# First graph parts of layer 1 issued beside the last outputs of layer 0, and one PSUM pool for both layers

## The chip, the cores and the metric

The kernel runs on one core of one Trainium2 chip. The metric is the device time of one execution in microseconds (us). The kernel before was executed three times, and the median of those three is its time. A profiled execution was taken beside them, with a trace of the instructions of each engine: PE (TensorE; PEld is its weight loads), DVE (VectorE), ACT (ScalarE), POOL (GpSimd) and SP (SyncE, which here issues most DMAs).

## The reference

Two graph layers over N = 3327 nodes with D = 256 features, all in float32. The adjacency matrix `adj` is N x N, and its entries are 0 or 1.

```python
# layer 0: graph attention, 4 heads of 64
h = relu(layernorm(x))
support = (h @ weight) per head
logits[h, n, m] = f1[h, m] + f2[h, n]          # two inner products of support
attn = softmax over m of leaky_relu(logits, 0.2) where adj[n, m] != 0
x = x + attn @ support + bias + h @ proj_w.T + proj_b

# layer 1: two steps of a graph mean beside a top-p attention
h = relu(layernorm(x))
R = row-normalized (adj + I);  Xf = Xa = h;  Z = 0
for n in range(2):
    A = rows of softmax((Xa W1' W2') (Xa W3')'), cut to the largest entries
        that hold 0.9 of the row, normalized again
    Xf = R @ Xf
    Xa = A @ Xa
    Z = Z + Xf @ U1[n].T + Xa @ U2[n].T
out = x + layernorm(h + Z)
```

## The kernel before

**Tiles.** The nodes make NT = 26 row tiles of 128 (the last has 127), and seven groups of up to four tiles (NG = 7; the seventh has two).

**Layer 0** goes over four blocks of 1024 columns (the last has 255), and in each block over the 26 row tiles: 104 steps. A step loads a tile of the transposed adjacency on SP's queue, writes it back to DRAM in the kernel's own copy `adj_r` on POOL's queue, and DVE weighs it once for each of the four heads (`weigh`, L570). The weighed tiles are `w`, from a ring of seven buffers. PE sums features (L578) and weights (L588) of all rows in PSUM. At a block's end the sums are copied to `ot`, and each of the block's row tiles gets an `Out` object with these pieces of work: `divide` (PE turns `ot`, L437), `normalize` (DVE divides, adds the residual and takes the statistics of the layer norm, POOL the root, ACT writes h, L464), `turn` (PE transposes h, L473), `keys` (L483, then `take_keys`), `graph` (PE multiplies by U1, L506; ACT copies the sums into the resident `xf0` and into `xu`, which SP stores in `p_d`) and `take_graph` (DVE's low part of `xf0`, L517, and stores). The outputs of the first three blocks are spread over the steps of the following block. The last block has just two row tiles, 24 and 25, and their outputs stand behind the loop, L683 to L694, with nothing else beside them: both divides and normalizes, a mean of the keys known so far, both turns, both keys, both graph products.

**Layer 1** handles one row tile in one iteration n, for n = -3 to 28, twice (steps s = 0 and 1). Several row tiles are in work at the same time, in roles from `m3` (queries loaded) over `m` (logits in seven pieces, L799, copied from PSUM by ACT or DVE, L810; then one exponential over the row, L822), `a` (probes that seek the threshold, L880), `b` (keep, L985) and `c` (transposes, L998, copies, L1008, and products with the features, L1019) to `d`. Their order is written out by hand, in six strings called PLANS. The R @ Xf of the step is cut into parts: `graph(i, s, ...)` is a generator that yields seven parts for row tile i. Each part loads a 128 x 4 x 128 piece of `adj_r` (`adjt`, a ring of ADJ = 3, issued by SP at L722) and issues eight matmuls on it (L742 and L743: high and low half of the features). Part 0 has two more with the identity; part 6 has two adjacency tiles and four matmuls. In part 3 the ends of the row tile before are forced and `ad` is loaded from `p_d`.

Each token `graph` in a plan adds `parts(s, n) / fills` to an amount due, where `fills` is 7, and issues a part whenever a whole one is due. In step 0 the iterations n = -1, 0 and 1 issue 3, 7 and 8 parts; the rest of the 182 is spread evenly over the other 24 iterations:

```python
even = (NG * NT - sum(PARTS[s].values())) / (LAST[s] - 2)
```

**Order.** The instructions of PE, DVE, ACT and POOL keep the order in which they are written in the program (`in_traced_order`). SP's order is the scheduler's.

**PSUM** has eight banks. Layer 0 takes them by number, `bank(k)`, from a pool of its own (`ps1`). That pool is closed, and layer 1 opens another (`ps2`) with named rings: `lg` 3 banks (logits, and the small products and transposes of roles c and d), `tr` 2 (transposes), `acca` 1 (product), `accr` 2 (graph).

Of the kernel before, what the change touches and what calls it, by code (L numbers as in the profile page):

```python
# [10 lines left out]
FP = mybir.dt.float32  # L11
FR = mybir.dt.float32r
# [42 lines left out]
def kernel(  # L55
# [126 lines left out]
    def queries_and_keys(xt, i, s, ptag, keys):  # L182


        pn = rows(i)
        pq = ps.tile([P, P], FP, tag=ptag, name="pq", bufs=3)
        for c in range(DC):
            nc.tensor.matmul(
                pq[:, :pn], wqk[:, c, :], xt[:, c, :pn], start=(c == 0), stop=(c == DC - 1)
            )  # L190
        yield
        t = small.tile([P, 2, P], FR, tag="qk", name="qk", bufs=1)
        yield from hi_and_lo(t, pq, i, s)
        nc.sync.dma_start(
            out=qk_d[s][:, :, i * P : i * P + pn].rearrange("v a n -> a v n"),
            in_=t[:, :, :pn].bitcast(FP),
        )
        if keys:
            take_keys(keys, t, i)
        yield  # L200
# [95 lines left out]
    right = kept.enter_context(tc.tile_pool(name="right", bufs=1, side="right"))  # L296
    pq = right
    res = right.tile([P, NT, D], FP, tag="xa", name="res")
    xf0 = new_graph(right)
    keys = new_keys(right)  # L300
    first_traced = len(nc.cur_bb.bb.instructions)
    with ExitStack() as l0:
        p0 = l0.enter_context(tc.tile_pool(name="p0", bufs=1))
        pa = l0.enter_context(tc.tile_pool(name="pa", bufs=2))
        ps = l0.enter_context(tc.tile_pool(name="ps1", bufs=1, space=PSUM))

        def bank(k, shape):
            return ps.tile(shape, FP, tag=f"b{k}", name="pt")

# [283 lines left out]

        ats = {}
# [14 lines left out]
        for step, (b, j) in enumerate(order):  # L609
# [11 lines left out]
            )  # L621
            i = j + AHEAD
# [41 lines left out]
            if b < NB - 1:  # L664
                last = b == NB - 2
                for k, r in enumerate(outs):
                    a = step + 1 + 3 * k
                    ka, kb, kc = ((3, 4)[k % 2], (5, 6)[k % 2], 7) if last else (6, 7, 6)
                    g = a + 5
                    for when, f in (  # L670
                        (a, lambda r=r, ka=ka: r.divide(ka)),
                        (a + (3 if last else 2), lambda r=r, kb=kb: r.turn(kb)),
                        (a + (4 if last else 3), lambda r=r, kb=kb: r.keys(kb)),
                        (g, lambda r=r, kc=kc: r.graph(kc)),
                    ):
                        on_pe.setdefault(when, []).append(f)
                    for when, f in (
                        (a + 1, r.normalize),
                        (a + (5 if last else 4), r.take_keys),
                        (g + 1, r.take_graph),  # L680
                    ):
                        on_dve.setdefault(when, []).append(f)
        for k, r in enumerate(outs):  # L683
            r.divide(k)
            r.normalize()
        mean_of_keys(keys, 0)
        for k, r in enumerate(outs):
            r.turn(2 + k)
# [21 lines left out]

    def graph(i, s, xf, ends):


        pn, n0 = rows(i), i * P
        acc = ps.tile([P, DX], FP, tag="accr", name="accr")
        dx = D if s else DX
        for g in range(NG):
            c0 = 4 * g
            a = pw.tile([P, 4, P], FR, tag="adjt", name="adjt", bufs=ADJ)
            cn = min(4, NT - c0)  # L720
            nf = min(cn, NF - c0)
            nc.sync.dma_start(  # L722
                out=a[:, :nf, :pn].bitcast(FP),
                in_=adj_r[c0 * P : (c0 + nf) * P, n0 : n0 + pn].rearrange("(c p) n -> p c n", p=P),
            )
            if nf < cn:
                move_rows(
                    nc.sync, a[:, nf, :pn].bitcast(FP), adj_r[NF * P :, n0 : n0 + pn], rows(NF)
                )
            if g == 3:  # L730
                while ends:
                    ends.pop(0)[1]()
                ad = pw.tile([P, D], FP, tag="ad", name="ad", bufs=1)
                move_rows(nc.sync, ad, (z_d if s else p_d)[n0 : n0 + pn], pn)

            todo = [(a[: rows(c0 + j), j, :pn], c0 + j) for j in range(cn)]
            if g == 0:
                todo.insert(0, (ident_r[:pn, :pn], i))
            for n, (w, c) in enumerate(todo):
                begin, end = g == 0 and n == 0, g == NG - 1 and n == len(todo) - 1  # L740
                xc = xf[c // HB][: rows(c), c % HB]
                nc.tensor.matmul(acc[:pn, :dx], w, xc[:, :dx], start=begin, stop=False)  # L742
                nc.tensor.matmul(acc[:pn, :D], w, xc[:, DX:], start=False, stop=end)  # L743
            if g < NG - 1:
                yield

        def add():
            if s == 0:
                nc.vector.reciprocal(rdeg[:pn, i : i + 1], acc[:pn, D : D + 1])
            nc.vector.scalar_tensor_tensor(  # L750
                ad[:pn], acc[:pn, :D], rdeg[:pn, i : i + 1], ad[:pn], ALU.mult, ALU.add
            )
            if s == STEPS - 1:
                move_rows(nc.sync, r_d[n0 : n0 + pn], ad, pn)

        def high():
            nc.scalar.copy(hl[:pn, 0], ad[:pn])

        def low():
            nc.vector.tensor_tensor(hl[:pn, 1], ad[:pn], hl[:pn, 0].bitcast(FP), ALU.subtract)  # L760
            move_rows(nc.sync, xf_d[s + 1][n0 : n0 + pn], hl.bitcast(FP), pn)

        ends.append(("dve", add))
        if s < STEPS - 1:
            hl = pw.tile([P, 2, D], FR, tag="hl", name="hl", bufs=1)
            ends += [("act", high), ("dve", low)]
        yield
# [3 lines left out]
    class Rows:  # L771
# [20 lines left out]
        def logits(r, k_sb, *pieces):  # L792
            pn = r.pn
            for p in pieces:
                m0 = p * 512
                mn = min(512, N + 1 - m0)
                r.pg[p] = ps.tile([P, 512], FP, tag="lg", name="pg", bufs=3)
# [194 lines left out]
        def transpose(r, *groups):  # L992
            for g in groups:
                if g == 0:
                    r.pt, r.wt = {}, {}
                r.pt[g] = ps.tile([P, 4, P], FP, tag="tr", name="pt")
# [16 lines left out]
        def product(r, xa, *groups):  # L1013
            for g in groups:
                if g == 0:
                    r.acc = ps.tile([P, D], FP, tag="acca", name="acca", bufs=1)
# [27 lines left out]
        def features_t(r):  # L1044
            r.ft = ps.tile([P, DC, P], FP, tag="lg", name="pt", bufs=3)
# [13 lines left out]
        def small_products(r, u_sb):  # L1059
            r.pz = ps.tile([P, 2, D], FP, tag="lg", name="pz", bufs=3)  # L1060
# [198 lines left out]
    )  # L1259
    LAST = (NT, NT - 1)  # L1260

    def parts(s, n):
        if n in PARTS[s]:
            return PARTS[s][n]
        even = (NG * NT - sum(PARTS[s].values())) / (LAST[s] - 2)
        return even if n < LAST[s] else 0.0

    with ExitStack() as fast:
        ps = fast.enter_context(tc.tile_pool(name="ps2", bufs=2, space=PSUM))
# [10 lines left out]
        graph_ends = []  # L1280

        def parts_of_graph(s, xf):
            for i in range(NT):
                yield from graph(i, s, xf, graph_ends)
# [89 lines left out]
    with ExitStack() as gen:  # L1374
        ps = gen.enter_context(tc.tile_pool(name="ps3", bufs=2, space=PSUM))
        pf = ps.tile([1, 1], FP, tag="lg", name="pf", bufs=3)
# [11 lines left out]
        with tc.If(lost_v > 0):  # L1388
            for s in range(STEPS):
                with ExitStack() as st:  # L1390
                    pc = st.enter_context(tc.tile_pool(name=f"gc{s}", bufs=1))
                    pw = st.enter_context(tc.tile_pool(name=f"gw{s}", bufs=1))
                    pq = pw
# [83 lines left out]
```

## Time and profile before

| | us |
|---|---|
| median of three executions | 2097.78 |
| lowest and highest | 2092.39 and 2099.72 |
| profiled execution, its own time | 2095.06 |
| span of its trace | 2092.8 |
| PE busy | 1985.8 (95%) |
| DVE busy | 1715.9 (82%) |
| ACT busy | 1265.2 (60%) |
| POOL busy | 787.5 (38%) |

The mean granted clock of TensorE in the profiled execution is 0.984 of full speed. Times inside the trace count from the start of its span. Layer 0 ends and layer 1 begins around 684 to 700 us; the last graph part of step 0 starts its last matmuls at 1382 (PE's rows of L742), and step 1 lasts from there to the end. In the listings, `L742` is line 742 of the kernel, `out<-in` are the program's names, `x6` is a number of instructions, and brackets give the idle time of the engine just before and what ended it. The profile's page has the span in 40 equal slices, with the busy share of each engine in tenths:

```profile
## 2 busy tenths in 40 slices
PE   6999999999999679999999999998899999999996
...
DVE  4777888878877388888888888864899999999995
ACT  2110000000012588888888888847899999999982
```

### The profile page before, as it was taken

What the parts mean: (1) busy time and instruction counts of PE and PEld (TensorE: products, weight loads), DVE (VectorE), ACT (ScalarE), POOL (GpSimd) and SP (SyncE); (2) the same over time, 40 slices, a digit from 0 to 9 for tenths busy, and PEclk for the clock granted to TensorE, in tenths of its full rate; (3) what the DMA queues carried; (4) which work ended last, traced back from release to release, by engine and by line L of the source; (5) the groups of instructions that cost most, each with busy time, mean ns of one, the idle gap of its engine ahead of it and who ended that gap; (6) DMA issues with size and microseconds to landing.
All of it is one profiled execution on the core that took longest, in us unless ns stands there. A gap on an engine that the chain in (4) does not pass through costs nothing. (4 is left out here: it accounts for less than half of the span.)

```text
span 2092.8 us, 34266 instructions
## 1 busy us (share of the span) xinstructions
PE 1985.8 (95%) x11474; PEld 1387.5 (66%) x11474; DVE 1715.9 (82%) x4065; ACT 1265.2 (60%) x1940; POOL 787.5 (38%) x1834
## 2 busy tenths in 40 slices
PE   6999999999999679999999999998899999999996
PEld 3333223323333468888888888876798898888885
DVE  4777888878877388888888888864899999999995
ACT  2110000000012588888888888847899999999982
POOL 2330033223233233444444444432555444554441
PEclk9999999999999889999999999999899999999998
DMA  5455555655645433333333333377334443334420
GB/s 173 146 174 170 161 196 190 229 175 183 217 131 175 130 81 91 102 100 98 102 102 103 100 103 103 101 224 197 77 99 102 118 105 102 101 99 111 107 73 20
DMA packets 319569, 270.60 MB, mean 129 GB/s; under 512 B 30168, under 2 KB 293335, under 8 KB 319256
## 3 DMA queue, kind: packets, MB, share of 16 engines
q1 hardware_dynamic: 303480, 216.03, 37.7%
q0 software_dynamic: 14736, 51.62, 7.0%
q8 instruction: 92, 1.51, 0.3%
q14 instruction: 93, 0.76, 0.1%
q10 hardware_dynamic: 1168, 0.67, 0.1%
HBM read 177.79 MB, written 88.62 MB: 127 GB/s over the span
## 5 line engine op out<-in xcount | busy, mean ns | idle before, releaser
L880 ACT ACTIVATE junk<-lg,at 128x3327 fp8e4<-128x3327 f32 (+1 forms) x208 | 637.8, 3067 | 13.8 <-POOL at L846 11.2
L570 DVE SCALAR_TENSOR_TENSOR w<-xf,cf,at 128x1024 f32<-128x1024 f32 (+1 forms) x312 | 382.1, 1278 | 55.9 <-PE pt L588 55.9
L742 PE MATMUL accr<-xf,adjt 128*128 128x258 f32 (+3 forms) x1352 | 366.8, 304 | 19.3 <-DMA adjt<-adj_r 18.9
L578 PE MATMUL pt<-w,sup 128*64 128x512 f32 (+3 forms) x1456 | 341.0, 576 | 10.6 <-DVE w L570 8.5
L743 PE MATMUL accr<-xf,adjt 128*128 128x256 f32 (+1 forms) x1352 | 340.6, 284 | 0.0
L1019 PE MATMUL acca<-res,wt 128*128 128x256 f32 (+2 forms) x1352 | 319.3, 381 | 0.0
L1019 PE MATMUL acca<-xa,wt 128*128 128x256 f32 (+2 forms) x1352 | 315.1, 382 | 3.0 <-ACT wt L1008 3.0
L742 PEld LDWEIGHTS accr<-xf,adjt 128*128 128x128 f32 (+1 forms) x1352 | 259.0, 192 | 29.9 <-DMA adjt<-adj_r 14.3
L1019 PEld LDWEIGHTS acca<-xa,wt 128*128 128x128 f32 (+2 forms) x1352 | 251.1, 191 | 34.7 <-ACT wt L1008 3.5
L1019 PEld LDWEIGHTS acca<-res,wt 128*128 128x128 f32 (+2 forms) x1352 | 249.2, 191 | 30.8 <-issue 0.5
L743 PEld LDWEIGHTS accr<-xf,adjt 128*128 128x128 f32 (+1 forms) x1352 | 259.8, 192 | 5.6
L799 PE MATMUL pg<-k_sb,q 128*128 128x512 f32 (+2 forms) x728 | 242.5, 425 | 17.3 <-DVE lg L810 8.4
L578 PEld LDWEIGHTS pt<-w,sup 128*64 128x64 f32 (+1 forms) x1456 | 95.9, 136 | 221.4 <-issue 149.2
L820 POOL TENSOR_SCALAR sc<-sc 128x1 f32<-128x1 f32 (+1 forms) x156 | 29.2, 215 | 505.0 <-ACT sc L818 505.0
L998 PE MATMUL pt<-ident,e 128*128 128x128 f32 (+1 forms) x1352 | 193.4, 276 | 20.8 <-DVE e L985 13.5
L946 DVE MAX8 v<-lg 128x8 f32<-128x416 f32 (+2 forms) x416 | 210.0, 577 | 0.1
L998 PEld LDWEIGHTS pt<-ident,e 128*128 128x128 f32 (+1 forms) x1352 | 162.8, 144 | 61.2 <-ACT wt L1008 18.1
L937 DVE SCALAR_TENSOR_TENSOR lg<-e,th 128x3327 f32<-128x3327 f32 (+1 forms) x52 | 191.1, 3676 | 4.1 <-ACT th L930 4.1
L985 DVE SCALAR_TENSOR_TENSOR e<-e,vm 128x3327 f32<-128x3327 f32 (+1 forms) x52 | 191.2, 3677 | 0.1
L822 ACT ACTIVATE e<-lg,sc 128x3327 f32<-128x3327 f32 (+1 forms) x52 | 159.7, 3072 | 29.9 <-issue 27.4
L1008 ACT COPY wt<-pt 128x512 f32<-128x512 f32 (+2 forms) x268 | 142.6, 544 | 55.7 <-PE pt L998 39.0
L588 PE MATMUL pt<-w,eas 128*32 128x512 f32 (+3 forms) x1456 | 166.6, 569 | 0.0
(180 smaller groups left out, 2696.1 us busy)
## 6 DMA issues: line engine op xcount, KB each, us to landing
adjt<-adj_r SPq DMA_DIRECT2D x300, 256.0 KB, 3.2
at<-in_adj_t_dram SPq DMA_DIRECT2D x75, 512.0 KB, 3.8
adj_r<-at POOLq DMA_DIRECT2D x75, 512.0 KB, 4.7
qk_d<-qk SPq DMA_DIRECT2D x50, 128.0 KB, 2.2
q<-qk_d SPq DMA_DIRECT2D x100, 64.0 KB, 2.5
xf_d<-xf SPq DMA_DIRECT2D x50, 128.0 KB, 2.5
xf_d<-hl SPq DMA_DIRECT2D x25, 256.0 KB, 2.0
xf<-f_d SPq DMA_DIRECT2D x24, 256.0 KB, 4.9
```

The source lines that it names most:

```text
L570: nc.vector.scalar_tensor_tensor(o, cb, cf[:pj, j, h : h + 1], a, ALU.max, ALU.mult)
L578: nc.tensor.matmul(acc[q * O : (q + 1) * O, :mn], sup[:pj, j, h * O : (h + 1) * O], ws[h][:pj, 512 * m : 512 * m + mn], start=(j == 0), st ...
L588: nc.tensor.matmul(acc[h * QP : (h + 1) * QP, :mn], eas[:pj, j, h : h + 1].to_broadcast([pj, QP]), ws[h][:pj, 512 * m : 512 * m + mn], sta ...
L742: nc.tensor.matmul(acc[:pn, :dx], w, xc[:, :dx], start=begin, stop=False)
L743: nc.tensor.matmul(acc[:pn, :D], w, xc[:, DX:], start=False, stop=end)
L799: nc.tensor.matmul(r.pg[p][:pn, :mn], r.q[:, v, :pn], k_sb[:, m0 : m0 + mn], start=(v == 0), stop=(v == 1),)
L880: nc.scalar.activation(junk[:pn], r.lg[:pn, :N], AF.Exp, bias=r.at[:pn, 4:], accum_out=r.g[:pn], saturate=False,)
L937: nc.vector.scalar_tensor_tensor(r.lg[:pn, :N], e, r.th[:pn], e, ALU.is_lt, ALU.mult, accum_out=r.below[:pn])
L946: nc.vector.max(r.v8[:pn, q], r.lg[:pn, q * w : min((q + 1) * w, N)])
L985: nc.vector.scalar_tensor_tensor(e, e, r.vm[:pn, 1:], e, ALU.is_ge, ALU.mult, accum_out=kept[:pn])
L998: nc.tensor.transpose(r.pt[g][: rows(c), j, : r.pn], r.e[: r.pn, c * P : c * P + rows(c)], ident[: r.pn, : r.pn],)
L1019: nc.tensor.matmul(r.acc[: r.pn], wt[: rows(c), j, : r.pn], xa[: rows(c), c, :], start=(c == 0), stop=(c == NT - 1),)
```

## The change

There are three edits.

1. **One PSUM pool.** It is opened before layer 0. Layer 0 takes banks by number as before. Layer 1's rings are fixed banks in round robin, counted per kind, and every `ps.tile(..., tag="lg")` and the like becomes `psum("lg", ...)`.
2. **Parts begun early.** `graph` and the load of a part (`load_part`) are defined before layer 0. Behind the loop of layer 0, after the last divides and normalizes and the mean of the keys, six parts of row tile 0 and two of row tile 1 are issued, ahead of the last two turns. The loads of the first three are issued in the last step of the loop and take their buffers from the ring of `w`, as the five others do. For these two row tiles, the ends of the row tile before and the load of `ad` come in part 6 and no longer in part 3.
3. **Quota.** These eight parts are subtracted (`DONE`), so that the 24 iterations share 156 parts and no longer 164. The iterations n = -1, 0 and 1 keep 3, 7 and 8.

```diff
+    ps = kept.enter_context(tc.tile_pool(name="ps", bufs=1, space=PSUM))
+    def bank(k, shape):
+        return ps.tile(shape, FP, tag=f"b{k}", name="pt")
+    BANKS = {"lg": (2, 3, 4), "tr": (0, 1), "acca": (5,), "accr": (6, 7)}
+    used = dict.fromkeys(BANKS, 0)
+    def psum(what, shape):
+        k = BANKS[what][used[what] % len(BANKS[what])]
+        used[what] += 1
+        return bank(k, shape)
...
+    BEGUN = 2
+    adjs = {}
+    def load_part(i, g):
+        pn, n0, c0 = rows(i), i * P, 4 * g
+        a = new_adj()
...
     def graph(i, s, xf, ends):
...
-        acc = ps.tile([P, DX], FP, tag="accr", name="accr")
+        acc = psum("accr", [P, DX])
...
-            a = pw.tile([P, 4, P], FR, tag="adjt", name="adjt", bufs=ADJ)
+            a = adjs.pop((i, g), None) or load_part(i, g)
...
-            if g == 3:
+            if g == (NG - 1 if i < BEGUN else 3):
                 while ends:
                     ends.pop(0)[1]()
                 ad = pw.tile([P, D], FP, tag="ad", name="ad", bufs=1)
                 move_rows(nc.sync, ad, (z_d if s else p_d)[n0 : n0 + pn], pn)
...
-        ps = l0.enter_context(tc.tile_pool(name="ps1", bufs=1, space=PSUM))
...
+        def new_adj():
+            return pa.tile([P, 4, P], FR, tag="w", name="adjt", bufs=7)
...
+            if step == len(order) - 1:
+                for g in range(3):
+                    adjs[0, g] = load_part(0, g)
             i = j + AHEAD
             weigh(j, at, b, cn, 0, 1)
...
+        graph_ends = []
+        begun = [graph(i, 0, xf0, graph_ends) for i in range(BEGUN)]
         for k, r in enumerate(outs):
             r.divide(k)
             r.normalize()
         mean_of_keys(keys, 0)
+        for part in range(EARLY // 4):
+            next(begun[0])
+        for part in range(2):
+            next(begun[1])
         for k, r in enumerate(outs):
             r.turn(2 + k)
...
-                r.pg[p] = ps.tile([P, 512], FP, tag="lg", name="pg", bufs=3)
+                r.pg[p] = psum("lg", [P, 512])
...
-                r.pt[g] = ps.tile([P, 4, P], FP, tag="tr", name="pt")
+                r.pt[g] = psum("tr", [P, 4, P])
...
-                    r.acc = ps.tile([P, D], FP, tag="acca", name="acca", bufs=1)
+                    r.acc = psum("acca", [P, D])
...
+    DONE = (EARLY // 4 + 2, 0)
...
-        even = (NG * NT - sum(PARTS[s].values())) / (LAST[s] - 2)
+        even = (NG * NT - DONE[s] - sum(PARTS[s].values())) / (LAST[s] - 2)
...
-        ps = fast.enter_context(tc.tile_pool(name="ps2", bufs=2, space=PSUM))
...
+        def new_adj():
+            return pw.tile([P, 4, P], FR, tag="adjt", name="adjt", bufs=ADJ)
 
         def parts_of_graph(s, xf):
             for i in range(NT):
-                yield from graph(i, s, xf, graph_ends)
+                yield from graph(i, s, xf, graph_ends) if s or i >= BEGUN else begun[i]
```

## The prediction, on record before the result

> **What bounds the kernel now.** I read the page's 40 slices first (layer 0 ends in slice 13, layer 1 begins), then one-microsecond windows and the timelines there, then the tile period behind it. The chain of waits reaches back only to 1487 us and says nothing of this place.
>
> Windows around the seam (columns: stretch, length, busy time of PE, PEld, DVE, ACT, POOL, granted clock, DMA share, GB/s):
>
> ```profile
> 684.00:685.00 1.00, 0.53 (x5) 0.33 (x4) 0.70 (x4) 0.00 (x0) 0.00 (x0) 1.00 0.79 266
> ...
> 687.00:688.00 1.00, 0.00 (x0) 0.00 (x0) 0.86 (x5) 0.28 (x1) 0.57 (x2) 0.96 0.00 0
> 688.00:689.00 1.00, 0.63 (x2) 0.29 (x2) 0.98 (x2) 0.32 (x1) 0.61 (x2) 0.50 0.00 0
> ...
> 693.00:694.00 1.00, 1.00 (x2) 0.34 (x1) 0.35 (x1) 0.10 (x1) 0.00 (x0) 0.50 0.13 33
> ...
> 708.00:710.00 2.00, 0.00 (x0) 0.01 (x1) 0.00 (x0) 0.27 (x1) 1.67 (x6) 0.60 0.73 177
> ```
>
> PE is empty after the last divide, comes back at half clock (0.50 up to 694), and is empty again to 710. The timelines of PE and ACT name the waits:
>
> ```profile
> 683.59 0.94 PE L437 MATMUL pt<-ident,ot 128*128 128x128 f32 x6 [1.01 <-ACT ot L659]
> 688.37 0.69 PE L473 MATMUL pt<-ident,res 128*128 128x128 f32 x2 [3.85 <-ACT res L464]
> 690.23 0.69 PE L473 MATMUL pt<-ident,res 127*128 127x127 f32 x2 [1.17 <-ACT res L464]
> ...
> 698.39 1.66 PE L799 MATMUL pg<-k_sb,q 128*128 128x512 f32 x6 [1.20 <-DVE xf L517]
> ...
> 710.02 0.55 PE L742 MATMUL accr<-xf,adjt 128*128 128x258 f32 x1 [5.83 <-DMA adjt<-adj_r]
> ```
> ```profile
> 700.47 0.58 ACT L810 COPY lg<-pg 128x512 f32<-128x512 f32 x1 [2.60 <-DMA p_d<-xu]
> ...
> 717.36 0.59 ACT L810 COPY lg<-pg 128x512 f32<-128x512 f32 x1 [2.73 <-PE pg L799]
> ```
>
> So layer 1 starts by a serial chain: turn (688.37), keys, graph products, the store of xu, first logits copied at 700.47. Behind 717.36 ACT has hardly a gap up to 746. Further on, in step 0's tiles (waits between 850 and 1350 us), the others wait for PE, and PE for nobody (one load of 0.90 us):
>
> ```profile
> ACT lg L810 <- PE pg L799: 38.1, 19, 2.6
> ...
> DVE nxa L1037 <- PE acca L1019: 19.8, 19, 1.5
> ```
>
> and its tiles follow at the pace of PE (starts of L822, one per tile):
>
> ```profile
> 1063.39 3.07 ACT L822 ACTIVATE e<-lg,sc 128x3327 f32<-128x3327 f32 x1
> ...
> 1089.36 3.07 ACT L822 ACTIVATE e<-lg,sc 128x3327 f32<-128x3327 f32 x1
> ...
> 1114.96 3.07 ACT L822 ACTIVATE e<-lg,sc 128x3327 f32<-128x3327 f32 x1
> ...
> 1140.46 3.07 ACT L822 ACTIVATE e<-lg,sc 128x3327 f32<-128x3327 f32 x1
> ```
>
> A tile with seven parts takes 25.97; where the quota 6.83 drops one part, two tiles take 25.60 and 25.50.
>
> **1. What leaves the tiles.** Parts in n = -1, 0, 1 stay 3, 7, 8. The other 24 tiles shared 182 - 18 = 164 parts (6.83), now 156 (6.50): eight parts fewer. One dropped part saved 2 x 25.97 - 51.10 = 0.84; again at 1244.38 to 1295.40: 51.02, 0.92; a third time (933.38 to 985.51: 52.13) nothing, since PE then waited 0.90 at 968.19 for an adjacency load. PE's own rows give 0.97 for a part (eight matmuls, 0.12 apart). Bounds: all like the third, 8 x -0.2 = -1.6 saved; at most 8 x 1.04 (1113.01 to 1114.05) = 8.3. I take 8 x 0.85 = **-6.8**, nearest to two of three rows.
>
> **2. What is added at the seam.** (a) Three adjacency tiles take slots of the seven w buffers, so all four weights of the last step wait for the sums of weights of the step before; now only the fourth does (678.31 behind PE L588). Four times 0.41 from 678.31 ends at 679.95, so the last sum of features starts about 680.1, not 679.44: +0.65. Behind these weights stand DVE's copy of ot and the divides, which move to 684.2 to 685.2.
> (b) Then 68 matmuls (parts 0 to 5 of tile 0: 50; parts 0 and 1 of tile 1: 18) stand on PE before the turn. At 0.12 and 0.4 for starts: 8.6 us, to 693.8. At 0.21, the spacing in the half-clock rows from 710, it would be 14.7. PE is busy at full clock before them with 1 us idle, so I take 8.6.
> (c) Their loads: three issue about 676.8 to 678 and land by 681 (median 3.2 us in the page's issue list). Five more follow in SP's queue between the stores: about 681.1, 682.5, 685.2, 686.5, 686.9, landing 684.3 to 690.1; PE wants them at 688.4, 689.5, 690.5, 691.6, 692.8. Cost 0; if each took the 7.0 of 702.94 to 709.9, the fifth would come at 693.9 and PE ends 1.2 later. The stores in SP's queue move by some 0.5 each for the loads passed, and none is what the turn waits for.
> (d) The turn moves from 688.37 to 693.8, +5.4. It took 12.1 us from turn to first logits copy, with 1.17 for the second normalization and half clock to 694.7. Now both inputs are ready and the clock full: turn and copy 0.95 (rows at 676.70 and 677.23), keys 2 x 0.65 (678.80), graph products 2 x 1.95 (680.59), two copies 0.75, the issue 0.35, landing 2.2 (697.90 to 700.11): 9.4, so 703.2, +2.75.
> (e) Of this some is swallowed. PE's 5.83 us wait at 710.02 was for a load queued behind two u_sb loads that land at 706.34 and 708.66. With SP 2.75 later they land about 711.3; the next part needed is now tile 0's last (128 KB, four matmuls) and not two full ones with the identity (18 matmuls at half clock). Logits of tile 1 come about 715, not 713.59; ACT, which waited 2.73 for them until 717.36, resumes **+1.5** late. Bounds: 0 if the shift is swallowed whole, +2.75 if none.
>
> **3. The common PSUM pool.** PE's 1.20 us wait at 698.39 (the new pool waiting for DVE's last read) goes: PE can start the logits at once, but their copies wait for the store of xu in any case, so 0. Banks now go round in fixed order. In step 1 a tile's piece 0 then follows DVE's copy of the previous piece 4: that ended at 1630.46 and PE started at 1630.67, elsewhere 0.55 to 0.85 apart. Cost 0, cover 0.2 at the least. In step 0 the swapped predecessors were read some 5 us before.
>
> **Sum:** -6.8 + 1.5 = -5.3. The profiled execution took 2095.06 (span 2092.8 and 2.3 around it): 2089.8. The median of the runs is 2.7 above it and would give 2092.5. I take the middle, **2091**.
>
> [...]
>
> **Rivals.**
> *A. The tiles don't shrink.* For: the third dropped part. With 6.5 the quota drops a part in every second tile, and each drop moves where the short part falls, so waits like 968.19 may come often. Then 0 saved: +1.5, middle 2097.9. Against: two of three drops paid.
> *B. The start is swallowed whole and the cold stretches shrink.* For: PE's gaps of 3.85 and 5.83 us are longer together than the 8.6 added. Then -8.3 + 0, middle 2088.
> *C. Slower: the fixed banks in step 1.* Its loop runs over 22 steady tiles of 23.8 to 24.0 us in which PE already waits for ACT and ACT's L822 waits 26.0 us in 21 tiles. If DVE's piece 4 ends later against PE than now, by more than the 0.2 to 0.85 of cover, each 0.1 us costs 2.2 us. At 0.5 past it: 11 - 5.3 = +5.7, 2102; from 0.24 on the gain is gone. Against: the cover is positive in each tile I looked at.
> *D. Slow start.* The 68 matmuls meet half clock or late loads: turn at 699.9, first copy some 9.8 late, 8.5 after swallowing: +1.7, middle 2098.
> That the parts stay where they were is excluded: PE keeps the written order, and the loads stand before the last stores in SP's queue.
>
> **Numbers.** Forecast 0.55, A 0.15, B 0.15, C 0.08, D 0.07. About 0.3% (6.3 us of 2097.78) is what a measurement of this kernel tells from no change; 2091.5 is that bound, in the middle of the forecast's own spread (2087 to 2095). Faster: 0.15 + half of 0.55 and a little, 0.45. Slower by 0.3%: C and the tails of A and D, 0.13. Same: 0.42. The range takes in B with its clock gains and C: 2083 to 2102.
>
> **What would show it.** Right: no idle on PE between 685 and 694 and clock 1.00 there; first logits copy about 703; L822 of tile 1 about 724 (722.36 now); step 0's tiles alternating so that two take 51.1, and L822 of the last tile 5 earlier than 1347.6; step 1 unchanged at 23.8 to 24.0. Wrong: waits for adjt in PE's rows between 685 and 694, tiles still at 25.97, or step 1 slower with PE waiting for DVE at L810.

## The result, and the profile after

The changed kernel took 2125.83 us (median of four runs, 2123.14 to 2127.87), the kernel before 2095.09 on the same chip (four runs). The ratio is 1.0144, with a 95% interval of 1.0118 to 1.0169: slower by 30.7 us, where 2091 and a range of 2083 to 2102 had been predicted. The profiled execution took 2126.55 us.

The page of the profile after, its second line (busy time, share of the span, instructions):

```profile
PE 1998.6 (94%) x11474; PEld 1397.3 (66%) x11474; DVE 1716.2 (81%) x4065; ACT 1265.8 (60%) x1940; POOL 805.9 (38%) x1834
```

DVE and ACT do what they did before, and PE is busy for 12.8 us more in a span that is 31.9 longer: the engines wait for each other. The place chosen for the new parts is not where the time went. Windows around the seam, the same stretches that were shown of before:

```profile
684.00:685.00 1.00, 0.96 (x8) 0.89 (x9) 0.45 (x3) 0.26 (x1) 0.00 (x0) 1.00 0.98 233
687.00:688.00 1.00, 1.00 (x11) 1.00 (x10) 0.96 (x5) 0.00 (x0) 0.81 (x3) 1.00 0.92 287
688.00:689.00 1.00, 1.00 (x11) 1.00 (x10) 0.90 (x3) 0.60 (x1) 0.36 (x2) 1.00 0.81 161
693.00:694.00 1.00, 0.70 (x7) 0.47 (x5) 0.00 (x0) 0.50 (x2) 0.00 (x0) 1.00 0.22 70
708.00:710.00 2.00, 0.26 (x1) 0.29 (x2) 0.02 (x1) 1.88 (x1) 0.30 (x2) 0.50 1.07 318
```

From 684.7 to 693 PE is full and its clock whole (1.00) where it stood empty and then ran at 0.50. The half clock hasn't gone, it comes later: from within a wait of PE of 3.69 us for the copies of the first logits on, the granted clock is 0.51 from 702 to 716 (before, 0.57 from 708 to 716). PE's and ACT's timelines of the changed kernel give the turn (L552), the first logits (L833), their copy (L844), and the first exponential of row tile 1 (L856, which was L822):

```profile
684.74 0.37 PE L358 MATMUL pt<-xf,ident_r 128*128 128x258 f32 x1
...
693.03 0.60 PE L552 MATMUL pt<-ident,res 128*128 128x128 f32 x4
...
709.74 0.55 PE L358 MATMUL pt<-xf,adjt 128*128 128x258 f32 x1 [1.93 <-DMA adjt<-adj_r]
```
```profile
702.96 0.58 ACT L844 COPY lg<-pt 128x512 f32<-128x512 f32 x1 [3.76 <-DMA p_d<-xu]
...
723.31 3.08 ACT L856 ACTIVATE e<-lg,sc 128x3327 f32<-128x3327 f32 x1
```

So the seam came out as predicted: 68 matmuls in 8.3 us (684.74 to 693.03), the first copy 2.5 late, tile 1 only 0.95 late. The loss lies behind it. Starts of the exponential over a row tile, one per tile:

| exponential | before | after | later by |
|---|---|---|---|
| step 0, tile 1 | 722.36 | 723.31 | 0.95 |
| tile 5 | 829.41 | 841.95 | 12.5 |
| tile 14 | 1063.39 | 1072.03 | 8.6 |
| tile 19 | 1192.40 | 1217.21 | 24.8 |
| tile 25, the last | 1347.60 | 1372.41 | 24.8 |
| step 1, tile 0 | 1425.17 | 1454.21 | 29.0 |
| tile 25 | 2014.54 | 2046.47 | 31.9 |

Between tiles 5 and 14 the tiles do shrink (867.68, 893.11, 918.67: two in 50.99, as foreseen). But two stretches, tiles 2 to 5 and 15 to 19, lose about 12 and 16 us. ACT's timeline in the second:

```profile
1125.46 3.07 ACT L856 ACTIVATE e<-lg,sc 128x3327 f32<-128x3327 f32 x1
...
1152.74 3.07 ACT L856 ACTIVATE e<-lg,sc 128x3327 f32<-128x3327 f32 x1
...
1184.03 3.07 ACT L856 ACTIVATE e<-lg,sc 128x3327 f32<-128x3327 f32 x1
...
1217.21 3.08 ACT L856 ACTIVATE e<-lg,sc 128x3327 f32<-128x3327 f32 x1
```

The tiles take 27.3, 31.3 and 33.2 us. What stands in the last of them is read engine by engine. DVE (L366 is `add` of a graph tile's ends, L376 its `low`, L1019 is `keep`):

```profile
1189.01 0.48 DVE L366 SCALAR_TENSOR_TENSOR ad<-pt,rdeg,ad 128x256 f32<-128x256 f32 x1
1194.32 0.43 DVE L376 TENSOR_TENSOR hl<-ad,hl 128x256 fp32r<-128x256 f32 x1 [4.82 <-ACT hl L373]
1194.66 3.68 DVE L1019 SCALAR_TENSOR_TENSOR e<-e,vm 128x3327 f32<-128x3327 f32 x1
```

ACT (L914 is a probe, L373 is `high`):

```profile
1190.82 3.08 ACT L914 ACTIVATE junk<-lg,at 128x3327 fp8e4<-128x3327 f32 x1
...
1193.88 0.40 ACT L373 CAST hl<-ad 128x256 fp32r<-128x256 f32 x1
```

PE (L1032, the transposes of the row that `keep` writes), and the window behind it:

```profile
1198.49 1.94 PE L1032 MATMUL pt<-ident,e 128*128 128x128 f32 x8 [4.45 <-DVE e L1019]
```
```profile
1197.00:1204.00 7.00, 5.51 (x20) 4.86 (x21) 5.87 (x18) 3.83 (x4) 1.80 (x3) 0.51 0.07 17
```

`add`, `high` and `low` stand together at one place of the written order. `low` waits 4.82 us on DVE, because `high` stands on ACT behind a copy of logits (from 1190.07) and a probe of 3.08; `keep` stands behind `low`, and PE's transposes wait 4.45 for `keep`. From 1197 to 1204 the granted clock is 0.51, and the eight transposes take 1.94 us, where eight such at 1136.62, with the clock at 1.00, take 1.06: so the wait is paid a second time in part. In the kernel before the three stood apart: `add` (there L750) at 1128.51 and `low` (L760) at 1133.11, with work of DVE's own between, and no wait:

```profile
1128.51 0.48 DVE L750 SCALAR_TENSOR_TENSOR ad<-accr,rdeg,ad 128x256 f32<-128x256 f32 x1
...
1133.11 0.42 DVE L760 TENSOR_TENSOR hl<-ad,hl 128x256 fp32r<-128x256 f32 x1
```

They stand together because part 3 of a graph tile forces what is left of the ends of the tile before (`while ends: ends.pop(0)[1]()`). The ends have places of their own in the plan, the tokens `ends.dve`, `ends.act`, `ends.dve`, all ahead of the seven tokens `graph`. Where a tile ends by the third of the seven, part 3 of the next tile comes within the same iteration and finds the ends still waiting. Counted from the written order: with 6.83 parts per iteration this happens at n = 1 and in no iteration from n = 2 on. With 6.50 the phase moves by half a part per iteration, and it happens at n = 0 to 3 and 13 to 17; at n = 2, 3, 16 and 17 at the last `graph` token, with a probe just ahead and `b.keep` behind. The exponential of tile k stands in iteration k - 1, ahead of those `graph` tokens, so what iteration n loses shows in the time up to the exponential of tile n + 2: tiles 2 to 5 and 15 to 19, just those that lose.

### The profile page after: what moved, and what is told of

Same layout as the page of the kernel before. It is cut to its first block, busy times and chain, and to the rows that moved or that the text cites. A ratio compares the mean times of both kernels' runs of the same rounds, so it can differ in the third digit from the quotient of the medians.

```text
span 2124.7 us, 34273 instructions
## 1 busy us (share of the span) xinstructions
PE 1998.6 (94%) x11474; PEld 1397.3 (66%) x11474; DVE 1716.2 (81%) x4065; ACT 1265.8 (60%) x1940; POOL 805.9 (38%) x1834
## 4 chain that ended last, share of the span: by engine, by line
PE 73%; ACT 13%; DVE 8%; issue 2%; DMA 2%; POOL 2%; SPq 0%; DVEq 0%; ACTq 0%; POOLq 0%
PE pt L1053 21%; PE pt L657 14%; ACT junk L914 8%; PE pt L667 7%; PE pt L1032 6%; PE pt L833 5%; PE pt L358 5%; PE pt L359 5%; PE pt L470 2%; PE pt L585 2%; ACT e L856 2%; PE pt L1096 2%; DVE e L1019 2%; DVE w L649 1%; DVE v L980 1%
## 5 line engine op out<-in xcount | busy, mean ns | idle before, releaser
L914 ACT ACTIVATE junk<-lg,at 128x3327 fp8e4<-128x3327 f32 (+1 forms) x208 | 637.8, 3067 | 16.1 <-POOL at L880 13.5
L358 PE MATMUL pt<-xf,adjt 128*128 128x258 f32 (+3 forms) x1352 | 367.5, 304 | 16.5 <-DMA adjt<-adj_r 16.3
L359 PE MATMUL pt<-xf,adjt 128*128 128x256 f32 (+1 forms) x1352 | 342.3, 285 | 0.0
L1053 PE MATMUL pt<-res,wt 128*128 128x256 f32 (+2 forms) x1352 | 320.3, 382 | 1.0 <-ACT wt L1042 1.0
L1053 PE MATMUL pt<-xa,wt 128*128 128x256 f32 (+2 forms) x1352 | 314.4, 381 | 2.3 <-ACT wt L1042 2.3
L358 PEld LDWEIGHTS pt<-xf,adjt 128*128 128x128 f32 (+1 forms) x1352 | 260.9, 193 | 27.9 <-DMA adjt<-adj_r 16.3
L1053 PEld LDWEIGHTS pt<-xa,wt 128*128 128x128 f32 (+2 forms) x1352 | 250.6, 191 | 34.1 <-ACT wt L1042 3.0
L1053 PEld LDWEIGHTS pt<-res,wt 128*128 128x128 f32 (+2 forms) x1352 | 249.7, 192 | 32.4 <-ACT wt L1042 2.1
L359 PEld LDWEIGHTS pt<-xf,adjt 128*128 128x128 f32 (+1 forms) x1352 | 261.5, 193 | 5.6
L833 PE MATMUL pt<-k_sb,q 128*128 128x512 f32 (+2 forms) x728 | 247.5, 434 | 18.6 <-ACT lg L844 10.2
L1032 PE MATMUL pt<-ident,e 128*128 128x128 f32 (+1 forms) x1352 | 198.1, 281 | 42.6 <-DVE e L1019 36.7
L854 POOL TENSOR_SCALAR sc<-sc 128x1 f32<-128x1 f32 (+1 forms) x156 | 29.2, 215 | 520.3 <-ACT sc L852 520.3
L1032 PEld LDWEIGHTS pt<-ident,e 128*128 128x128 f32 (+1 forms) x1352 | 166.8, 147 | 84.9 <-issue 35.6
L1019 DVE SCALAR_TENSOR_TENSOR e<-e,vm 128x3327 f32<-128x3327 f32 (+1 forms) x52 | 191.2, 3678 | 0.1
L856 ACT ACTIVATE e<-lg,sc 128x3327 f32<-128x3327 f32 (+1 forms) x52 | 159.7, 3072 | 29.4 <-issue 27.1
```

The lines of the kernel that those rows point to most:

```text
L833: nc.tensor.matmul(r.pg[p][:pn, :mn], r.q[:, v, :pn], k_sb[:, m0 : m0 + mn], start=(v == 0), stop=(v == 1),)
L856: nc.scalar.activation(r.e[:pn], r.lg[:pn, :N], AF.Exp, bias=nmu[:pn], accum_out=r.ssum[:pn])
L914: nc.scalar.activation(junk[:pn], r.lg[:pn, :N], AF.Exp, bias=r.at[:pn, 4:], accum_out=r.g[:pn], saturate=False,)
L1019: nc.vector.scalar_tensor_tensor(e, e, r.vm[:pn, 1:], e, ALU.is_ge, ALU.mult, accum_out=kept[:pn])
L1032: nc.tensor.transpose(r.pt[g][: rows(c), j, : r.pn], r.e[: r.pn, c * P : c * P + rows(c)], ident[: r.pn, : r.pn],)
L1053: nc.tensor.matmul(r.acc[: r.pn], wt[: rows(c), j, : r.pn], xa[: rows(c), c, :], start=(c == 0), stop=(c == NT - 1),)
```

## The experiments

Theory **T**: the forced ends cost it, and the quota's phase brings them about. Rivals: **R1**, adjacency loads that come late (case A of the prediction); **R2**, the fixed PSUM banks (case C); **R3**, the begun parts themselves.

| kernel | median, us | ratio to before | interval |
|---|---|---|---|
| the change | 2125.83 | 1.0144 | 1.0118 to 1.0169 |
| e1, ends forced in part 6 | 2092.46 | 0.9987 | 0.9978 to 0.9996 |
| e2, begun parts with the old quota | 2100.85 | 1.0028 | 1.0018 to 1.0038 |
| e3, the quota alone | 2122.28 | 1.0127 | 1.0112 to 1.0141 |
| e4, the pool alone | 2095.03 | 1.0001 | 0.9993 to 1.0010 |
| e5, e1 with the reloads first | 2093.96 | 0.9997 | 0.9988 to 1.0006 |
| e6, the quota with the late force | 2093.02 | 0.9994 | 0.9983 to 1.0005 |
| e7, before, forced in part 1 | 2142.63 | 1.0219 | 1.0201 to 1.0238 |
| e8, before with the reloads first | 2099.74 | 1.0020 | 1.0010 to 1.0030 |
| e9, the change with `high` on DVE | 2095.80 | 1.0001 | 0.9991 to 1.0012 |
| e10, e1 with the parts around the turn | 2090.26 | 0.9978 | 0.9968 to 0.9989 |
| e11, e10 with early keys | 2087.43 | 0.9969 | 0.9957 to 0.9981 |
| e12, before with early keys | 2097.74 | 1.0023 | 1.0014 to 1.0032 |

### e1: ends forced later

```diff
-            if g == (NG - 1 if i < BEGUN else 3):
+            if g == (3 if s else NG - 1):
```

> The changed kernel, but in step 0 the ends of a row tile are forced in part 6 of the next one (as the change has it for tiles 0 and 1), not in part 3. Theory T (forced ends): the eight parts fewer move the phase of the quota, so that in iterations n = 2, 3 and 13 to 17 a row tile's last part and part 3 of the next come in the same iteration; part 3 then forces add, high and low at one place, DVE waits for ACT (4.8 us at n = 17) ahead of its keep, and PE's transposes wait for that. With the later force all ends come by their own tokens: no wait of DVE's low for ACT over 1.5 us from n = 2 on, tile periods of 25.4 to 25.6 throughout n = 5 to 23, and the 9 us lost at tiles 4 and 5 and the 17 us lost at tiles 15 to 19 are back: about 2125.8 - 27 = 2099, 2094 to 2103. Rival R1 (late adjacency loads, since each drop moves where the short part falls): the loads stand where they stood, 2120 to 2128. Rival R2 (fixed PSUM banks hold up PE in step 0): the banks are the same, 2120 to 2128.

33.4 us came back with one line (1.5 more than T's range had it), and banks, adjacency loads, quota and begun parts stayed. The line also moves the load of `ad`, which stands in the same branch; so it does in e6 and e7, and e9 below leaves it where it was. Three rows of waits, each with the total in us, the number of times and the longest. The first two are the changed kernel's (DVE between 690 and 1360, PE between 830 and 1360), the third is e1's (PE between 830 and 1330):

```profile
DVE hl L376 <- ACT hl L373: 23.4, 9, 4.8
```
```profile
PE pt L1032 <- DVE e L1019: 12.3, 5, 4.5
```
```profile
PE pt L358 <- DMA adjt<-adj_r: 1.6, 2, 1.1
```

In e1 PE waits for nothing else there, and on DVE no wait for `high` is left:

```profile
1171.46 0.48 DVE L366 SCALAR_TENSOR_TENSOR ad<-pt,rdeg,ad 128x256 f32<-128x256 f32 x1
1176.24 0.42 DVE L376 TENSOR_TENSOR hl<-ad,hl 128x256 fp32r<-128x256 f32 x1
```

The two are 4.8 us apart (5.3 in the changed kernel), but DVE works in between. Tile by tile, the changed kernel's periods over those of e1 sum to 33.4 as well: 15.6 at tiles 2 to 5, 16.7 at tiles 15 to 19, 1.1 at tile 20. PE's waits for adjacency loads between 830 and 1360 are as long in e1 as in the changed kernel (1.6 and 1.7 us in all). R1 and R2 fall as causes of the loss.

### e3 and e6: the quota alone

Both start from the kernel before, with its two pools and without a begun part. e6 has the late force besides.

```diff
-        {-3: 0, -2: 0, -1: 3, 0: 7, 1: 8},
+        {-3: 0, -2: 0, -1: 7, 0: 9, 1: 10},
```

> The kernel before, with two PSUM pools and no begun part; only the numbers of parts in n = -1, 0 and 1 are 7, 9 and 10 instead of 3, 7 and 8, so that the other 24 iterations share 156 parts (6.50) in the same phase as in the changed kernel. T: the same ends are forced at n = 2, 3 and 13 to 17, DVE's low waits for ACT some 4 to 5 us at n = 2, 3, 16 and 17, and it is slower than before by 20 to 30 us from these places, and up to 5 by the fuller start: 2115 to 2130. R1 and R2 and R3, which need the begun parts or the pool: no loss there, 2090 to 2102.

> The kernel before (two pools, no begun part) with 7, 9 and 10 parts in n = -1, 0 and 1, so 6.50 in the others, as in the third experiment, and the late force in step 0. T: the 20 to 30 us of the third experiment vanish with the forced ends, tile periods of 25.4 to 25.6 in n = 5 to 15, 2092 to 2098. The begun parts' own worth is then the difference from the first experiment: tile 1's first exponential at 725.4 here against 723.3, so some 2 us. Rival (what the quota costs are late adjacency loads): 2115 and more.

e3 is slower by 1.27%, with nothing in it of the change but its quota, and with it the phase (its start is fuller). Its waits between 690 and 1330:

```profile
DVE hl L760 <- ACT hl L757: 23.0, 8, 4.8
```
```profile
PE pt L998 <- DVE e L985: 21.3, 8, 4.5
```

Its tiles 15 to 19 take 27.11, 26.31, 27.29, 31.20 and 33.11 us, those of the changed kernel 27.10, 26.32, 27.29, 31.28 and 33.18. The late force takes 29.3 us from it (e6). R3 falls. Against e6, the begun parts of e1 bring tile 5 forward by 3.85 us (826.32 against 830.17); the medians differ by 0.6, where some 2 had been expected, and these intervals don't separate them.

### e7: the forced end by itself

```diff
-            if g == 3:
+            if g == (3 if s else 1):
```

> The kernel before with one number changed: in step 0 the ends are forced in part 1 of the next row tile, not in part 3. Quota, parts, loads and banks stay. By the written order the ends are then forced at n = 2 to 7 with the graph token ahead of the next probe, and at n = 8 to 13 with the last graph token, just ahead of b.keep. T: at n = 8 to 13 each costs what it costs in the changed kernel at n = 2, 3, 16 and 17 (5.7 to 7.6 us), at n = 2 to 7 each 0.7 to 1.7: 38 to 55 us slower in all, 2130 to 2150. Rivals R1 (loads) and R2 (banks): nothing of theirs is touched, so 2092 to 2099.

The kernel before, with one number changed, becomes slower than the change. Tiles 5 to 9 take 27.06 us each, 1.1 over 25.97 for an end forced ahead of the next probe; tiles 10 to 15, with the ends forced at the last token, take 32.44, 33.77, 32.25, 33.19, 33.65 and 32.21, on average 6.95 over 25.97. Tile 4, the first with an end forced by the new rule, takes 27.78 and loses nothing: it took 28.32 before. 5 x 1.1 + 6 x 6.95 = 47.2. By the profiles tile 25 is 45.9 late (1393.51) and step 1's tile 25 49.2 (2063.69); the medians differ by 49.3. PE's waits between 900 and 1140 us:

```profile
PE pt L998 <- DVE e L985: 28.0, 7, 4.7
```

### e9: who is waited for

```diff
-            nc.scalar.copy(hl[:pn, 0], ad[:pn])
+            nc.vector.tensor_copy(hl[:pn, 0], ad[:pn])
```

> The changed kernel with its force in part 3, its quota, banks and begun parts; only the high half of a row tile's features (the copy between add and low) is made by DVE and not by ACT. The ends are then forced at the same places, but DVE does add, high and low in a row and waits for nobody. T, first reading (the price is DVE's wait for ACT, 4.8 us ahead of keep, and PE's idle time and half clock behind it): the losses at n = 2, 3 and 13 to 17 go but for some 0.5 us each, 2093 to 2103. Second reading (the price is DVE's own work standing ahead of keep, or part 3 itself): 2118 to 2128.

The first reading holds: with the ends forced at the very same places, 30.0 us are back. DVE's timeline at n = 17, the place shown of the changed kernel:

```profile
1165.87 0.48 DVE L366 SCALAR_TENSOR_TENSOR ad<-pt,rdeg,ad 128x256 f32<-128x256 f32 x1
1166.39 0.29 DVE L373 CAST hl<-ad 128x256 fp32r<-128x256 f32 x1
1166.72 0.43 DVE L376 TENSOR_TENSOR hl<-ad,hl 128x256 fp32r<-128x256 f32 x1
1167.06 3.68 DVE L1019 SCALAR_TENSOR_TENSOR e<-e,vm 128x3327 f32<-128x3327 f32 x1
```

From `add` to `keep` it is 1.2 us and not 5.65. So the price was the way to ACT and back at a place where ACT had a probe in front.

### e4 and e2: the pool, and the begun parts with the old quota

e4 is the kernel before with the common pool alone. e2 is the change with 2, 4 and 4 parts in n = -1, 0 and 1:

```diff
-        {-3: 0, -2: 0, -1: 3, 0: 7, 1: 8},
+        {-3: 0, -2: 0, -1: 2, 0: 4, 1: 4},
```

> The kernel before with only the common PSUM pool and its fixed banks; quota and parts are as before. T: 2092 to 2099, tile periods as before in both steps, and the passage from step 0 to step 1 (first exponentials 77.6 us apart) within 2 us of before. R2: what the changed kernel loses is the banks, so 2110 to 2128, or at least the 7 us that the changed kernel loses in the passage to step 1 and its first three tiles.

> The changed kernel, but the eight begun parts are taken from the iterations n = -1, 0 and 1, which issue 2, 4 and 4 instead of 3, 7 and 8; the other 24 share 164 as before (6.83), with the same phase against the row tiles as before. T: no forced end from n = 2 on, so the losses at tiles 4, 5 and 15 to 19 vanish though begun parts, loads and banks stay; tiles of 25.97 as before, and up to 8 parts (7 us) less work at the start, part of it idle there anyway: 2089 to 2099. R1: the loads of the begun parts, or the ring behind them, disturb later loads: somewhere over 2110. R2 (fixed banks): 2115 to 2128. R3 (the begun parts on PE cost the start more than they give): tile 1's first exponential more than 3 us later than in the changed kernel.

e4 follows the kernel before within 0.3 us at each exponential of step 0, and the medians are 0.2 apart: no cost of the pool shows. In e2 the losses at tiles 4, 5 and 15 to 19 are gone as T has it (tile 25 is 0.96 late), but it ends above T's 2099: its passage to step 1 is 2.3 us longer than in the kernel before, and the four tiles behind it take 2.7 more. Eight parts fewer at the start also gained nothing: tile 5 is 1.3 late. Between 722 and 835 PE waits 25.4 us in e2 and 17.7 in the kernel before, so what the missing parts free goes into waiting; and DVE's `add` waits 2.9 us there for `ad`, whose load now stands in part 6, just ahead of it. How much each binds there isn't separated.

### e10: the begun parts around the turn

e10 has e1's line and, beside it, this:

```diff
-        for part in range(EARLY // 4):
-            next(begun[0])
-        for part in range(2):
-            next(begun[1])
+        for part in range(4):
+            next(begun[0])
         for k, r in enumerate(outs):
             r.turn(2 + k)
...
             r.graph(k)
             r.take_graph()
+        for part in range(2):
+            next(begun[0])
+        for part in range(2):
+            next(begun[1])
```

> The changed kernel with the late force of the first experiment, and the begun parts split: four of them ahead of the two turns and four behind the two graph products, not all eight ahead of the turns. By the prediction's step 2 the turn waits 5.4 us for 68 matmuls, of which 3.85 us fit in the gap that was there; four parts (34 matmuls, 4.1 us) fill that gap alone, and the other four stand in the time in which PE waited for the store of xu and the copies of the first logits. Theory S: the turn at 689.0 to 690.0 instead of 693.0, the first logits copied at 699.5 to 701.5 (702.96 in the first experiment), tile 1's first exponential 1.5 to 3 us earlier, so 2089.5 to 2091.5. Rival: the start is bound by the adjacency loads behind, and tile 1 comes at 722.5 to 723.5 as before: 2092 to 2094.

PE and ACT of e10:

```profile
690.08 0.40 PE L552 MATMUL pt<-ident,res 128*128 128x128 f32 x2
691.91 0.44 PE L552 MATMUL pt<-ident,res 127*128 127x127 f32 x2 [1.42 <-ACT res L543]
```
```profile
701.85 0.59 ACT L846 COPY lg<-pt 128x512 f32<-128x512 f32 x1 [4.16 <-DMA xf_d<-xf]
...
721.41 3.07 ACT L858 ACTIVATE e<-lg,sc 128x3327 f32<-128x3327 f32 x1
```

The turn comes 2.95 us earlier than in the changed kernel, tile 1 1.9 earlier, and with that earlier than in the kernel before too (722.36). The turn and the first copy are a little outside S's ranges (to 690.0 and to 701.5), the copy because it now waits for the store of the features, which PE's parts don't touch. This is the change as it was meant, and faster than before by 0.2%; its interval overlaps e1's, but its tile 25 is 2.6 us earlier than e1's (1336.21 and 1338.85).

### e5, e8, e11, e12: where the rest of the gain stays

By the last exponential of step 0, e1 is 8.75 us ahead of the kernel before, and at the end 2.4 by the medians. The passage between the steps takes 81.47 us in e1 (first exponential of step 1 behind the last of step 0), and 77.57 before. Theory P: DVE's `keep` now starts just ahead of POOL's checks, the reloads of the graph's features wait behind these, and the keys land late. e5 (on e1) and e8 (on the kernel before) issue the checks behind the reloads:

```diff
                     graphs, filled = parts_of_graph(s + 1, load_graph(right, s + 1)), False
+                    held.make_sure()
...
-                        if what[0] == "queries":
+                        if what[0] == "make_sure" and n == NT - 1 and not end:
+                            held = tiles[s, i]
+                        elif what[0] == "queries":
```

> The changed kernel with the late force of the first experiment, and one more edit: in iteration n = 25 of step 0, POOL's four checks for role b (make_sure) are issued behind the reloads of the graph's features for step 1, not ahead of them. Theory P (the passage): the late force gained 8.75 us by the last exponential of step 0 and kept 2.4, because DVE's 3.7 us keep came just ahead of POOL's checks, the fourth of which then ended with it; the reloads started 32.0 us behind the last exponential instead of 29.2, the keys queued behind them landed later (66.5 and not 64.6), PE idled and its clock halved. With the reloads first they start about 25 to 27 behind the last exponential, the keys land by 64, and the 81.5 us from the last exponential of step 0 to the first of step 1 become 76 to 78: 2086 to 2090. Rival: the passage is set by the amount moved (6 MB at the full share of the DMA engines) and not by the start of the reloads: 81 us again, 2091 to 2094.

> The kernel before with only the edit of the passage: POOL's checks for role b in iteration n = 25 of step 0 are issued behind the reloads. P: reloads start 25 to 27 us behind the last exponential, not 29.2; the keys land 2 to 4 us earlier and so does the first exponential of step 1: 2090 to 2093, against 2094.9. Rival: 2094 to 2096.

P falls. The reloads start at 24.7 (e5) and 25.1 (e8) behind the last exponential, not 32.0 and 29.2, but the keys land at 65.0 and 65.7 (66.5 in e1 and 64.6 in the kernel before), the passages are 81.0 and 81.1, and e8 is slower than before. Then the keys themselves, on e10 and on the kernel before (`load_keys` takes the columns as a last argument):

```diff
+                    next_keys = new_keys(right)
+                    load_keys(next_keys, s + 1, 0, (0, (EARLY - 2) * P))
                     graphs, filled = parts_of_graph(s + 1, load_graph(right, s + 1)), False
-                    next_keys = new_keys(right)
...
-                    load_keys(next_keys, s + 1, 0)
+                    load_keys(next_keys, s + 1, 0, ((EARLY - 2) * P, EARLY * P))
```

> The split kernel of the experiment before, with one edit at the passage from step 0 to step 1: of the keys of step 1, the columns of the first 22 row tiles are loaded at the start of iteration n = 26, ahead of the reloads of the graph's features, and only tiles 22 and 23 one iteration later. Theory K: from the last exponential of step 0 on, the chain is the store of tile 23's keys, the load of all keys (landing 65 to 67 us behind the last exponential in every kernel so far, whether the reloads start at 25 or at 32), DVE's mean over them, and what stands behind it on DVE; the 5 us of gain that the late force lost lie here. With most keys loaded early the rest lands by 58 to 62, and the first exponential of step 1 comes 75 to 79 us behind the last of step 0, not 81.9: 2084 to 2088. Rival: the 6 MB of reloads set the passage (the parts of step 1 need them), 81 to 83 us again, 2089 to 2092.

> The kernel before with only the early load of the first 22 row tiles' keys. K: the passage of 77.6 us becomes 72 to 75, 2089 to 2092. If the changed quota's 5 us in the passage come by way of the keys, the passages of this kernel and of the one beside it are now within 1.5 us of each other; if they come by another way, the difference of 3 to 4 us stays. Rival (the reloads): 2093 to 2096.

DVE's mean over the keys (L262), and the scaling behind it (L1073), in the kernel before and in e11:

```profile
1412.29 3.35 DVE L262 TENSOR_REDUCE mean<-k_sb 128x1 f32<-128x3072 f32 x1 [11.64 <-DMA k_sb<-qk_d]
```
```profile
1396.03 3.35 DVE L262 TENSOR_REDUCE mean<-k_sb 128x1 f32<-128x3072 f32 x1 [5.97 <-DMA k_sb<-qk_d]
...
1405.91 0.48 DVE L1073 TENSOR_SCALAR nxa<-pt,rk 127x256 f32<-127x256 f32 x1 [6.27 <-PE pt L1055]
```

In e11 the mean starts 60.3 us behind the last exponential (67.1 in e10), and then DVE waits 6.27 for PE's last product: the wait changed its owner. The passage is 79.36, 2.6 less, and e11 has the lowest median of all (its interval overlaps e10's). K's 75 to 79 was just missed, its 2084 to 2088 met. The same edit makes the kernel before slower (e12, passage 80.10 and not 72 to 75, 2097.74 and not 2089 to 2092), though its mean starts 61.6 us behind the last exponential and not 64.7; K does not explain that. The two passages lie within 0.8 us of each other, as K's reading by way of the keys asks, but as e12's came there by growing, that shows nothing for K. And e12's profile also has tile 5 at 826.30, 3.1 earlier than the kernel before, though PE, DVE, ACT and POOL have the same written order up to n = 25, so one profile of it carries no more than that. **What makes the passage 77.57 us in the kernel before and 78.8 to 82.2 in all the others stays open.** With what follows in step 1 it is 4 to 7 us of the changed kernel's loss in its profile, and it is left in e1 too, so it is no part of the 33.4. Each kernel has one profile, and the 26 executions of the kernel before that were run beside e1 to e4 lie between 2091.02 and 2098.99 us, so the differences between these passages may in part be those of single executions.

## Why the prediction was wrong

- **Step 1, what leaves the tiles (-6.8): the step that failed.** What it counted was of a fair size: without the forced ends, e1 gains 9.7 us on the kernel before between tile 1 and tile 25, 5.7 of them at tiles 6 to 25; in the other 4.0, at tiles 2 to 5, parts and the ends that the kernel before forces at n = 1 aren't separated. But the step priced the dropped part as PE's time alone, with a late load as its only risk (case A). A quota is also a phase: it sets at which token a row tile ends, and the tile's end has work on three engines tied to it. With the phase moved, `low` waited for ACT, `keep` for `low`, and PE for `keep`. That the tokens and the force in part 3 depend on this could be read in the code, by counting parts for n = 2 to 25 under both quotas. The term left out measured +33.4 us, where the bounds of step 1 allowed a loss of 1.6 at most. At tile 25 the profile agrees: 0.95 - 9.7 + 33.4 = 24.7, and 24.8 was measured.
- **The passage to step 1 and the tiles behind it, put at nothing ("step 1 unchanged").** They are the rest of the 31.9: the passage 4.2 longer, and 2.9 more by step 1's tile 25, most of it in the first four tiles. The cause stays open.
- **Step 2, the seam (+1.5): right.** (a) The divides moved by 0.45 (683.59 to 684.04; 684.2 foreseen). (b) 8.3 us for the 68 matmuls against 8.6. That the clock would stay full was the author's estimate; from 684 to 694 it was 1.00. (c) No wait for a load among them. (d) First copy at 702.96 against 703.2. (e) Tile 1 0.95 late against 1.5. That the turn need not pay was not seen: e10 places the same parts so that tile 1 comes before its old time.
- **Step 3, the pool (0): right**, by e4. Case C had no part in it, and step 1's steady tiles stayed at 23.8 to 24.3 us.
- **The rivals.** None of the four named this mechanism. Case A looked in the right place, the drops, and named the wrong wait: PE's waits for adjacency loads between 830 and 1360 us are 1.7 us in all in the changed kernel, against 12.3 for `keep`. The 0.13 for slower came from C and from tails, and the range ended 24 us short.
- **Matmuls in written order**, as (b) and (d) count them: both turns' inputs were ready on ACT at 690.64, and they started behind the parts at 693.03. What the prediction didn't ask is the same of DVE and ACT. Row: `keep` started at 1194.66, though DVE had made its own inputs by 1186.9, since `low` stood waiting in front of it from 1189.5. On ACT `high` started at 1193.88, behind the probe, though `add` had ended on DVE at 1189.5. So in the changed kernel the forced ends put DVE's queue behind ACT's (23.4 us in nine waits of `low` for `high`); in e9, where `high` is DVE's, no such wait is left.

## What to carry to other kernels

Where work is handed out by a fractional quota beside a fixed order, a change of the quota is a change of phase: count, for every iteration, which event falls at which place, before pricing the quantity. Where two engines pass a small piece back and forth (DVE, ACT, DVE) at one place of the written order, the first waits for whatever stands ahead of the middle step (here DVE 4.82 us, with ACT's probe of 3.08 ahead of `high`): give the steps places apart, or make one engine do all three, which took 1.2 us here from `add` to `keep` where the exchange took 5.65. And work put into a gap is free only up to the gap's length: here 8.3 us of parts in a gap of 3.85 moved the turn by 4.66; in e10, split over two gaps, it brought tile 1 forward by 1.9 us.

## What the runs showed of the hardware

Where PE waited some 4 us for `keep`, the tile grew by more than the wait. In e7 PE's seven waits of this kind between 900 and 1140 sum to 28.0 us, the longest 4.7, and six tiles took 6.95 us longer on average; the granted clock was 0.87 to 0.95 over such tiles (944 to 1103, in five windows), and 1.00 in the kernel before (1082 to 1108). In the changed kernel the clock was half (0.50) for 3.4 us behind the wait of 4.47 that ended at 1166.27, and for 6.8 us from within the one of 4.45 that ended at 1198.49; behind the wait of 1.12 that ended at 1136.62 it stayed at 1.00.

In e1, POOL's fourth check at 1367.37 ended only at 1370.91, while DVE's `keep` ran from 1367.19 to 1370.86; the reload behind it on POOL started at 1370.86 as well. In the kernel before the check took 0.19 us from 1376.21, ahead of `keep` at 1376.42. What held the check in e1 was not shown: no run here tried it alone.
